# Both state products of the second scan on GpSimd, six state buffers, sums three states behind

## The chip, the cores and the metric

The kernel runs on one core of one Trainium2 chip. The metric is the device time of one execution in microseconds (us). Before the change three runs took 2472.06, 2475.49 and 2479.26 us; their median is 2475.49 us.

In the text PE is TensorE (the matmul engine; PEld its weight loads), DVE is VectorE, ACT is ScalarE, POOL is GpSimd and SP is the engine whose queue issues the DMAs.

## The reference, cut to what matters

A decoder of four layers works on x of shape (4, 256, 256). Each layer has an attention, a cross-attention and a feed-forward part, each added to x and normalised. The first two layers' cross-attentions are selective scans over a context; only the second (layer 1) is meant by "the second attention's loop" here, because its scan runs beside that layer's self-attention:

```python
# layer 1, "xattn": b = 4 batches, l = 256 steps, e = 256 channels, n = 16 states per channel
u     = silu(conv(in_proj(ctx)))                  # (b, e, l)
Bm,Cm = x_proj(u)                                 # (b, 16, l) each
delta = softplus(dt_proj(...) + dt_proj_b)        # (b, e, l)
A     = -exp(A_log)                               # (e, 16)
state_n[t] = state_n[t-1] * exp(delta[t] * A[:, n]) + (delta * u)[t] * Bm[n, t]
y[t]  = sum over n of state_n[t] * Cm[n, t]
out   = (y + D * u) * silu(x_normed)
```

So there are 4 x 16 = 64 scans of 256 channels by 256 steps. Each needs a product with B before it (call it product 1), and a product with C after it (product 2); sixteen results are summed per batch.

## The kernel before

Channels lie on the 128 partitions; a state tile `s` holds 2 x 256 = 512 numbers per partition (two halves of the channels). `Scans._steps` is a generator that the other parts advance: each `next` emits one state. For state (b, n) it emits, in this order:

- L511-512, `add`: the sum of an older state. `late` holds states whose sum has not been emitted; when more than one waits, the oldest is added by a matmul with the identity into a PSUM bank (`ssmps`; two instructions on PE, L500). So sums run two states behind. After n = 15 the bank is folded into `u` (L504).
- L514: a DMA from the SP queue brings row n of B and of C, broadcast to 128 partitions, into `bc` (256 KB; four buffers).
- L518: ACT makes exp(delta A) in one of three `dA` tiles, in two instructions.
- L520: product 1, `s = du * B`, on DVE (helper `tt`, L111), or on POOL (helper `ptt`, L123) when `self.apart` is set.
- L521: the scan on DVE, in place in `s`.
- L529: product 2, `s = s * C`, on DVE (L111).

The tile `s` has four buffers (`wk` has bufs=4); `xd` in the prologue shares its tag. A buffer is free again when PE has summed its state. The `bc` buffer is free again after product 2.

The first scan (layer 0) runs beside the first attention, `run_mqa`, two states per step of its loop, with both products on DVE. The second scan begins in the tail of that; 24 of its states are emitted in layer 0's feed-forward part (L749), 8 in the prologue of the second attention (`run_gqa`, L1031). Then L1035 sets `apart`, and the loop `SmallHeads.run` (L960-972) emits the last 32 states, one per step, with product 1 on POOL.

A step of that loop: PE computes one group of score matmuls for row maxima (`sc`, four instructions; 32 groups in all, 11 of them ahead of the loop) interleaved with one group of transposed scores (`sT`); ACT takes exp of `sT` (`e`); DVE takes two maxima from `sc` (`qn`, L129); then the state of the scan is emitted; then, every second step, PE multiplies `e` with ones and with the values (`o`), and every fourth step DVE takes a reciprocal of 128x256 and a product (`rec`, `oT`, L916). Three PSUM buffers hold `sc`, so PE's next group needs DVE's maxima. For each batch the output projection is added to `x` and normalised (`settle`), and some steps later `gate_pair` (L535) multiplies the scan's `y` by silu(x), transposes the product on PE (L545), adds it to `x` and normalises again. A normalisation asks POOL for the root (`rstd`: L169 and a two-column power through L123), and DVE then scales x (L117). `gate_pair`'s product (L541) is on POOL too. So POOL's queue holds product 1 of the states, the roots and the gate products.

Each engine runs its queue in order. The order in a queue is made when the program is built, by a scheduler that goes by the order of the program, by free buffers and by its own estimates of durations; it may put a later state's work ahead of something that is not ready by its estimate.

Of the kernel before, what the change touches and what calls it, by code (L numbers as in the profile page):

```python
# [19 lines left out]
F32 = mybir.dt.float32  # L20
# [9 lines left out]
ADD, SUB, MUL, MAX, MIN = ALU.add, ALU.subtract, ALU.mult, ALU.max, ALU.min  # L30

P = 128
B, L, D = 4, 256, 256
NT = B * L // P
DC = D // P
# [170 lines left out]
def again(ap, n):  # L206

    return ap.unsqueeze(1).to_broadcast([ap.shape[0], n, ap.shape[1]])
# [189 lines left out]
class Scans:  # L398
# [44 lines left out]
    def _steps(self, pre):  # L443
        K, nc, w, wk = self.K, self.K.nc, self.w[pre], self.wk
        cols = w["cols"]
        N = B * L
        u = self.one.tile([P, DC, N], F32, name="u", bufs=2)
        delta = self.one.tile([P, DC, N], F32, name="delta")
        du = self.one.tile([P, DC, N], F32, name="du")


        taps = []
        for j in range(4):
            t = wk.tile([P, D], F32, name="tap", tag="bc", padded_shape=[P, 2 * L])
            nc.sync.dma_start(out=t, in_=K.A[f"{pre}_cw"][:, j * D : (j + 1) * D].to_broadcast([P, D]))
            K.ptt(t, t, w["in"], MUL)
            taps.append(t)
        for h in range(2):
            for c in range(DC):
                ps = self.bank()  # L460
                for j in range(4):
                    K.mm(ps, taps[j][:, c * P : (c + 1) * P], K.ctxp[:, 2 * h : 2 * h + 2, j : j + L], j == 0, j == 3)
                K.act(u[:, c, 512 * h : 512 * h + 512], ps, AF.Identity, bias=cols[:, c, 0:1])
        K.act(u, u, AF.Silu)
        negA = self.one.tile([P, DC, 16], F32, name="negA")
        K.act(negA, cols[:, :, 2:18], AF.Exp)
        K.ts(negA, negA, -1.0, None, MUL)
        bc = self.dram.tile([2, 16, N], F32, name="bcd")
        for h in range(2):
            s = slice(512 * h, 512 * h + 512)  # L470
            xd = wk.tile([P, 512], F32, name="xd", tag="s")
            ps = self.bank()
            for c in range(DC):
                K.mm(ps[0:40, :], w["xp"][:, c, :], u[:, c, s], c == 0, c == DC - 1)
            nc.scalar.copy(xd[0:40, :], ps[0:40, :])
            for k in range(2):
                nc.sync.dma_start(out=bc[k, :, s], in_=xd[8 + 16 * k : 24 + 16 * k, :])
            for c in range(DC):
                ps = self.bank()
                K.mm(ps, w["dt"][:, c * P : (c + 1) * P], xd[0:8, :])  # L480

                K.ts(delta[:, c, s], ps, cols[:, c, 1:2], None, ADD)
                K.act(du[:, c, s], ps, AF.Abs, bias=cols[:, c, 1:2])
        K.act(du, du, AF.Exp, scale=-1.0)
        K.act(du, du, AF.Ln, bias=K.eps[1.0])
        for c in range(DC):
            K.stt(delta[:, c, :], delta[:, c, :], 0.0, du[:, c, :], MAX, ADD)
            K.ptt(du[:, c, :], delta[:, c, :], u[:, c, :], MUL)

        turn = 0  # L490
        self.y = u

        late = []
        bank = {}

        def add(b, n, s):
            if n == 0:
                bank[b] = self.bank()
            y = bank[b]
            K.mm(y, K.ident, s.rearrange("p c l -> p (c l)"), n == 0, n == 15)  # L500
            if n == 15:
                for c in range(DC):
                    v = u[:, c, b * L : (b + 1) * L]
                    K.stt(v, v, cols[:, c, 18:19], y[:, c * L : (c + 1) * L], MUL, ADD)  # L504
                self.done += 1

        for b in range(B):
            lo = b * L
            for n in range(16):
                yield  # L510
                if len(late) > 1:  # L511
                    add(*late.pop(0))
                t = wk.tile([P, 2, L], F32, name="bc", tag="bc")
                nc.sync.dma_start(out=t, in_=bc[:, n, lo : lo + L].unsqueeze(0).to_broadcast([P, 2, L]))  # L514
                dA = self.dA[turn % 3]
                turn += 1
                for c in range(DC):
                    K.act(dA[:, c, 1:L], delta[:, c, lo + 1 : lo + L], AF.Exp, scale=negA[:, c, n : n + 1])  # L518
                s = wk.tile([P, DC, L], F32, name="s")
                (K.ptt if self.apart else K.tt)(s, du[:, :, lo : lo + L], again(t[:, 0, :], DC), MUL)  # L520
                nc.vector.tensor_tensor_scan(  # L521
                    out=s.rearrange("p c l -> p (c l)"),
                    data0=dA.rearrange("p c l -> p (c l)"),
                    data1=s.rearrange("p c l -> p (c l)"),
                    initial=0.0,
                    op0=MUL,
                    op1=ADD,
                )
                K.tt(s, s, again(t[:, 1, :], DC), MUL)  # L529
                late.append((b, n, s))  # L530
        for t in late:
            add(*t)
# [1907 lines left out]
```

## Time and profile before

| | |
|---|---|
| median of three runs | 2475.49 us (2472.06 to 2479.26) |
| the profiled execution | 2469.83 us |
| its span | 2468.1 us |
| mean granted TensorE clock | 0.948 |
| PE busy over the span | 2265.7 us (92%) |
| DVE busy | 1457.9 us (59%) |
| ACT busy | 801.0 us (32%) |
| POOL busy | 383.2 us (16%) |
| the 32 products 1 on POOL | first at 576.9 us, last at 734.4 us |
| the 128 scans (both layers) | first at 86.5 us, last at 735.7 us |

The span is the time between the first and last instruction of the profiled execution; 1.7 us of its time lie outside. "Busy" of PE is the union of its matmuls, whose ends are modelled. The granted clock is what the throttle let TensorE have; 1.00 is full speed.

### The profile page before, as it was taken

Reading aid. Unit: us, or ns where it says so; the run is one execution under the profiler, and the core shown is the slowest. Engines: PE = TensorE matmul, PEld = TensorE weight load, DVE = VectorE, ACT = ScalarE, POOL = GpSimd, SP = SyncE. Lnnn points to the kernel's source line nnn. Section 1 sums busy time; section 2 is a strip of 40 time slices with the busy share of each in tenths; the row PEclk is TensorE's granted clock in tenths of the full one; section 3 lists DMA queues with packets and bytes.
Section 4 is the critical chain, followed back from the end, with each engine's and each line's share of the span. In section 5 each row is a group of like instructions: output and inputs, shape, how many; then the busy total and the mean of one; then the engine's idle time right before and its main releaser. Section 6 shows DMA issues by size and latency. Waiting matters only on the chain. (4 is left out here: it accounts for less than half of the span.)

```text
span 2468.1 us, 28762 instructions
## 1 busy us (share of the span) xinstructions
PE 2265.7 (92%) x10624; PEld 1521.6 (62%) x10624; DVE 1457.9 (59%) x2920; ACT 801.0 (32%) x1781; POOL 383.2 (16%) x521
## 2 busy tenths in 40 slices
PE   8889998659986999899999999999999988899997
PEld 4466664325434655536888888888776543476774
DVE  3799983788875211280455444444556677774566
ACT  4567663523441111162211111111122243343434
POOL 2221214132330322200011000100210002100001
PEclk9999997778887999999999999999988899999999
DMA  6222221322213544220222112110100002100000
GB/s 201 60 60 59 53 52 35 70 48 50 52 39 101 164 131 127 78 77 9 73 82 87 45 46 73 45 63 31 46 22 1 20 18 71 41 1 1 1 1 18
DMA packets 132836, 138.99 MB, mean 56 GB/s; under 512 B 13876, under 2 KB 120726, under 8 KB 130904
## 3 DMA queue, kind: packets, MB, share of 16 engines
q1 hardware_dynamic: 132696, 137.16, 19.1%
q8 instruction: 84, 1.38, 0.2%
q14 instruction: 56, 0.46, 0.1%
HBM read 134.27 MB, written 2.85 MB: 56 GB/s over the span
## 5 line engine op out<-in xcount | busy, mean ns | idle before, releaser
L132 PE MATMUL ps<-xw,xcT 128*128 128x256 f32 (+1 forms) x2304 | 518.9, 382 | 0.3 <-ACT YT L126 0.3
L132 PEld LDWEIGHTS ps<-xw,xcT 128*128 128x128 f32 x2304 | 430.8, 190 | 64.0 <-issue 1.9
L132 PE MATMUL sc<-kT,qT 32*128 32x256 f32 (+2 forms) x1024 | 239.1, 403 | 11.7 <-DVE qn L129 11.3
L132 PEld LDWEIGHTS sc<-kT,qT 128*128 128x128 f32 (+1 forms) x1024 | 151.7, 200 | 89.7 <-issue 53.5
L111 DVE TENSOR_TENSOR xp<-ps,xb 128x256 f32<-128x256 f32 x96 | 40.4, 421 | 229.7 <-PE ps L132 229.6
L521 DVE TENSOR_TENSOR_SCAN s<-dA,s 128x512 f32<-128x512 f32 x128 | 160.2, 1266 | 15.4 <-POOL s L123 15.3
L132 PE MATMUL ssmps<-s,idz 128*128 128x512 f32 x256 | 142.8, 664 | 24.9 <-DVE s L111 24.0
L126 ACT ACTIVATE dA<-delta,negA 128x255 f32<-128x255 f32 x256 | 116.6, 501 | 133.7 <-DVE s L521 133.6
L126 ACT ACTIVATE p<-sc,nm 128x256 f32<-128x256 f32 (+1 forms) x256 | 111.8, 444 | 101.5 <-DVE nm L129 96.3
L111 DVE TENSOR_TENSOR hT<-u,a 128x512 f32<-128x512 f32 x48 | 33.2, 691 | 186.1 <-PE u L132 186.1
L132 PE MATMUL o<-pT,vt 128*128 128x256 f32 (+1 forms) x352 | 115.0, 449 | 15.5 <-ACT pT L332 15.1
L126 ACT ACTIVATE sq<-xp 128x1024 f32<-128x1024 f32 x24 | 25.4, 1057 | 314.3 <-DVE xp L111 314.3
L129 DVE TENSOR_REDUCE qn<-sc 128x2 f32<-128x480 f32 (+1 forms) x192 | 87.1, 506 | 40.1 <-PE sc L132 38.4
L123 POOL TENSOR_TENSOR xp<-xp,rn 128x128 f32<-128x128 f32 x96 | 35.2, 403 | 476.9 <-DVE rn L1408 476.9
L126 ACT ACTIVATE e<-sT 128x512 f32<-128x512 f32 x128 | 70.2, 590 | 107.7 <-PE sT L132 106.5
L129 DVE TENSOR_REDUCE nm<-sc 128x2 f32<-128x512 f32 (+1 forms) x128 | 76.7, 612 | 45.8 <-PE sc L132 45.5
L1476 DVE TENSOR_TENSOR_SCAN dec<-xT,idz 128x256 f32<-128x256 f32 (+1 forms) x192 | 89.8, 536 | 22.1 <-DMA xT<-ad 22.1
L132 PE MATMUL sT<-q,kT 32*128 32x256 f32 (+1 forms) x384 | 98.7, 501 | 1.7 <-ACT e L126 1.5
L169 POOL TENSOR_SCALAR rstd<-mv 128x2 f32<-128x2 f32 x48 | 11.7, 245 | 555.1 <-DVE mv L161 545.2
L126 ACT ACTIVATE a<-g 128x512 f32<-128x512 f32 x48 | 28.7, 597 | 206.9 <-PE g L132 206.8
L132 PE MATMUL g<-xT,wj 128*128 128x512 f32 x192 | 92.1, 603 | 0.7 <-ACT rows L100 0.7
L123 POOL TENSOR_TENSOR hT<-hT,sel 128x512 f32<-128x512 f32 x48 | 60.7, 1267 | 202.1 <-DVE hT L111 101.1
(504 smaller groups left out, 4133.2 us busy)
## 6 DMA issues: line engine op xcount, KB each, us to landing
bc<-bcd SPq DMA_DIRECT2D x128, 256.0 KB, 4.6
xw<-in_l2a_xw_dram SPq DMA_DIRECT2D x24, 768.0 KB, 4.9
xT<-ad SPq DMA_DIRECT2D x12, 1024.0 KB, 4.6
wj<-in_l1f_gate_dram SPq DMA_DIRECT2D x48, 128.0 KB, 2.5
wj<-in_l1f_up_dram SPq DMA_DIRECT2D x48, 128.0 KB, 2.8
wj<-in_l1f_down_dram SPq DMA_DIRECT2D x48, 128.0 KB, 2.9
sel<-cwd SPq DMA_DIRECT2D x32, 192.0 KB, 3.1
sel<-cwd SPq DMA_DIRECT2D x32, 128.0 KB, 3.2
```

Of the source, the lines that this page charges most:

```text
L111: self.nc.vector.tensor_tensor(out=out, in0=a, in1=b, op=op)
L123: self.nc.gpsimd.tensor_tensor(out=out, in0=a, in1=b, op=op)
L126: self.nc.scalar.activation(out, in_, func, **kw)
L129: self.nc.vector.tensor_reduce(out=out, in_=in_, axis=AX.X, op=op, **kw)
L132: self.nc.tensor.matmul(out, lhsT=lhsT, rhs=rhs, start=start, stop=stop)
L169: self.nc.gpsimd.tensor_scalar(out=out, in0=in_, scalar1=add, scalar2=None, op0=ADD)
L521: nc.vector.tensor_tensor_scan(out=s.rearrange("p c l -> p (c l)"), data0=dA.rearrange("p c l -> p (c l)"), data1=s.rearrange("p c l -> p ...
L1476: nc.vector.tensor_tensor_scan(out=dec[:, k, h, :], data0=ap[:, h, at(bb, k, j) : at(bb, k, 2)], data1=K.idz[:, 0 : (2 - j) * P], initial=0.0,
```

## The change

Inside the second attention's loop (where `apart` is set) product 2 goes to POOL as product 1 does, and a state's sum is emitted three states later, not two. The tile `s` has six buffers, not four; since the buffers are the pool's, this holds for both scans, from the first attention on. `xd` shares the tag and gets the same number. Elsewhere both products stay on DVE and sums stay two states behind.

```diff
@@ Scans._steps
-            xd = wk.tile([P, 512], F32, name="xd", tag="s")
+            xd = wk.tile([P, 512], F32, name="xd", tag="s", bufs=6)
...
-                if len(late) > 1:
+                if len(late) > (2 if self.apart else 1):
                     add(*late.pop(0))
...
-                s = wk.tile([P, DC, L], F32, name="s")
-                (K.ptt if self.apart else K.tt)(s, du[:, :, lo : lo + L], again(t[:, 0, :], DC), MUL)
+                s = wk.tile([P, DC, L], F32, name="s", bufs=6)
+                product = K.ptt if self.apart else K.tt
+                product(s, du[:, :, lo : lo + L], again(t[:, 0, :], DC), MUL)
                 nc.vector.tensor_tensor_scan(
...
-                K.tt(s, s, again(t[:, 1, :], DC), MUL)
+                product(s, s, again(t[:, 1, :], DC), MUL)
                 late.append((b, n, s))
```

## The prediction

> **What bounds the kernel now.** I read the page first: PE is busy 92% of the span, and all 32 states that the change moves lie between 576.9 and 735.7 us. Then the windows view, cut at the stages:
>
> ```profile
> core 0: us, PE busy (x) PEld busy (x) DVE busy (x) ACT busy (x) POOL busy (x), PEclk, DMA share, GB/s
> 86.00:330.00 244.00, 216.86 (x926) 149.12 (x925) 238.34 (x353) 159.80 (x454) 48.50 (x37) 0.99 0.24 59
> ...
> 577.00:690.00 113.00, 108.72 (x689) 54.42 (x688) 94.36 (x137) 48.29 (x96) 33.08 (x30) 0.88 0.24 55
> 690.00:747.00 57.00, 49.01 (x292) 19.37 (x288) 39.37 (x57) 24.55 (x44) 19.02 (x18) 0.88 0.13 32
> ```
>
> In the first attention (86 to 330 us) DVE is full, 238.34 of 244 us. In the second (577 to 747 us) PE is: 157.7 of 170 us, against 133.7 for DVE and 52.1 for POOL. So at most 12.3 us, PE's idle time, can be had there, unless the clock changes: it was granted at 0.88, and halved stretches moving about are worth some us either way. Next the waits between 575 and 740 us (us in total, times, longest):
>
> ```profile
> POOL s L123 <- PE ssmps L132: 89.5, 25, 15.9
> ...
> DVE s L521 <- POOL s L123: 15.3, 14, 2.3
> ...
> DVE x L117 <- POOL rstd L123: 5.1, 5, 1.1
> ...
> PE sc L132 <- DVE qn L129: 4.2, 6, 1.2
> ...
> PE ps L545 <- POOL gate L123: 3.3, 1, 3.3
> ```
>
> POOL's long wait is for a free buffer: product 1 starts when PE has summed the state four before it. DVE's scan waits for that product; the maxima queued behind the scan make PE wait, but for 4.2 us only. The timeline, engine by engine, shows one turn:
>
> ```profile
> 604.16 1.12 PE L132 MATMUL ssmps<-s,idz 128*128 128x512 f32 x2
> 604.26 1.29 DVE L129 TENSOR_REDUCE qn<-sc 128x2 f32<-128x512 f32 x2 [0.33 <-PE sc L132]
> ...
> 605.37 1.26 POOL L123 TENSOR_TENSOR s<-du,bc 128x512 f32<-128x512 f32 x1 [3.42 <-PE ssmps L132]
> ...
> 606.66 1.22 DVE L521 TENSOR_TENSOR_SCAN s<-dA,s 128x512 f32<-128x512 f32 x1 [1.11 <-POOL s L123]
> ...
> 607.92 0.69 DVE L111 TENSOR_TENSOR s<-s,bc 128x512 f32<-128x512 f32 x1
> ```
>
> Sum ends (605.28), product 1 to 606.63, scan to 607.88, product 2 to 608.61, and only then the next maxima (608.53). PE's groups abut all the while: a pair of steps takes from 602.24 to 610.06, 7.8 us or 3.9 us a step at full clock, without a gap.
>
> **The change part by part.** *Product 2 leaves DVE*: 32 x 0.69 = 22 us off DVE. This is not on PE's path except where maxima are late. *It goes to POOL*: no row has it there; product 1 has the same shape and kind, two SBUF inputs of 128x512, 1.27 us (1.26 to 1.68 in all rows). From below, DVE's 0.69; from above, 1.68. I take 1.27: POOL gets 32 x 1.27 = 41 us, 93 of 170.
>
> *A collision*, from the timeline near 645 us:
>
> ```profile
> 645.54 1.27 POOL L123 TENSOR_TENSOR s<-du,bc 128x512 f32<-128x512 f32 x1
> 645.61 1.68 DVE L117 TENSOR_SCALAR x<-x,mv,rstd 128x256 f32<-128x256 f32 x2 [1.14 <-POOL rstd L123]
> ...
> 648.02 1.26 POOL L123 TENSOR_TENSOR gate<-gate,u 128x512 f32<-128x512 f32 x1 [1.21 <-ACT gate L126]
> ...
> 648.40 1.96 DVE L521 TENSOR_TENSOR_SCAN s<-dA,s 128x512 f32<-128x512 f32 x1
> ```
>
> A scan beside a POOL product took 1.96 us against its usual 1.22, losing 0.74 of the 0.88 us that they shared; the two scalings of x took 1.68, and 0.73 at 740.12 with POOL idle. The maxima, read from PSUM, took 1.28 for two beside a product at 613.79, no more than alone. So I count two products and a scan of a state one after the other: 2 x 1.27 + 1.22 = 3.76 us. PE's step is 3.9: it fits, by 0.14. The Trainium skill, "SBUF — State Buffer", section "SBUF: two separate sides", goes further: VectorE operations with two SBUF inputs, or in a two-port mode, and GpSimd share an exclusive port pair, and the loser waits for the whole instruction. By the rule a state takes the full 3.76 us whatever the order; by the row 0.14 of each 0.88 us shared is kept, some 3.6 us, so the fit in PE's step would be 0.14 by the one and 0.3 by the other. It speaks against the change: products on POOL do not run free beside DVE's scans.
>
> *One turn again.* With six buffers and sums three behind, product 1 may again start when the sum of that step ends, now one state further ahead; the same lock-step. Counted from 604.26 (0): product 1 1.1 to 2.4, scan to 3.6, product 2 on POOL to 4.9, the next product 1 (free at 4.1 by PE) to 6.2, its scan to 7.4. Before, DVE came free of that second turn at 7.5 (611.06 + 0.69). So POOL's second turn comes 0.8 us later and gives back the 0.69 that DVE saves: zero, from -0.7 if the scheduler puts the next product 1 first, to +0.7 if it slips another half product. PE hides both signs unless a step is short of slack.
>
> *Reciprocal steps.* Pairs with `rec` and `oT` (2.17 us on DVE) took 9.3 us (610.06 to 619.37) for 7.8 plus 0.4 of transposes: PE loses 1.1 us, five times up to 700 us. `o` ends at 610.16, before the new scan can start: the reciprocal may now go first, and the maxima come 1.1 us earlier. Gain 0 to 5.5 us; I take 2, since DVE's order decides.
>
> *POOL's other work.* Behind product 2, which waits for a scan, POOL's queue holds the next product 1, six roots (0.22 + 0.71) and three gate products. DVE's x (L117), then ACT's gate, then PE's transposes (L545) wait for those. A root can meet a product just begun: 0 to 1.27 us; a product starting behind it can hold x for 0.95 (1.68 - 0.73), as twice or three times already. Charged to PE where it stalls on the gate, three times: 3 x (0 to 2.2) = 0 to 6.6; I take 3.
>
> *The last steps.* After 690 us no maxima remain. Undisturbed, PE's pair of steps took 7.0 us (722.00 to 728.96, with a projection of 1.0), 3.0 to 3.5 a step, less than POOL's 3.76. Over 11 states that is 11 x 0.3 to 0.7, 3 to 8 us; three states of lead (3 x 3.76 = 11 us) and the stalls at the gate cover it. Charge 0, 8 without cover.
>
> *Sums three behind*: the same 64 matmuls; one more at the tail, 1.1 us, while PE at 747 waits for the last gate anyway: zero, 1.1 uncovered.
>
> *The `bc` load* now waits for POOL: on SP nothing urgent stands behind it before 747 us. The state multiplied at 608.34 freed its tile at 611.75, the fourth after it was multiplied at 625.47: 13.7 us for a load of 4.6. Two us later is hidden; zero.
>
> *Six buffers in the first attention*: DVE idle is 5.7 of 244 us, so reordering gains at most that and can lose as much by an earlier scan before a maximum; I take 0.
>
> Sum: -2 + 3 = +1 us on 2469.83, of a size with nothing. On the median of the runs, 5.7 us above the profiled execution: 2476. A measurement of this kernel can tell about 0.3%, 7.4 us, from no change.
>
> **The rivals.** *Slower:* the queue of POOL paces. It decides if products and scan take more than PE's step, 3.9 us, that is, if each state slips by over 0.14 us; then the scan stands blocked in DVE's queue with the maxima or the reciprocal behind it and PE stops. Price: six roots at 2.2 us = 13, or the uncovered last steps 8 with the gates' 6.6; 8 to 20 us in all, 2484 to 2495. For: 3.76 is close to 3.9, and DVE already waits 1.1 us for POOL in every second step. Against: at half clock PE's steps are twice as long, and three states of lead absorb a slip.
>
> *Faster:* DVE's 22 us do reach PE. Then the reciprocals give 5.5 and the other gaps before `sc` and the gate part of the 12.3 us: -8 to -12, 2463 to 2468. For: DVE had 79% to carry, and its order loosens. Against: PE has only 12.3 us to give, and 6 of them sit in gate chains that POOL lengthens.
>
> *It does not do what it says:* the scheduler keeps the states two ahead, since `dA` has three tiles; then the lead is not there but neither is the collision, within 3 us of now; counted with no change.
>
> **How the numbers follow.** No change 0.50, with its own range 2469 to 2483 (2476 -+ 7); slower 0.29; faster 0.21. The range from 2463 to 2493 leaves out the far end of the slower case and what no row shows.
>
> **What would show it.** Right: after, `s<-s,bc` on POOL 32 times at about 1.27 us; DVE busy between 577 and 747 down some 22 us; PE's busy sum there unchanged near 158 us, the stretch 170 -+ 7; POOL's wait for `ssmps` replaced by waits for scans; DVE's wait for `s` above 15 us. Wrong: PE's waits for `qn` or for the gate growing past 15 us (slower), or gone (faster); a shift of over 5 us before 575 us, which I charge nothing.

## The result and the profile after

The changed kernel takes 2481.86 us in the median of 22 runs (2474.33 to 2499.15); the kernel before takes 2475.28 us beside it (22 runs, 2467.87 to 2483.35). The ratio is 1.0036, with a 95% interval of 1.0020 to 1.0052: some 9 us slower in the mean (6.6 between the medians), a little over what can be told from no change. The profiled execution took 2492.25 us, its span 2490.5, at a granted clock of 0.935; before it was 2469.83 us at 0.948.

So a part of the distance between the two profiles is the clock. Over all timed runs of this study, compared within each kernel, the time rises by 0.32 us for each us of half-speed clock (half-speed time being 2 x (1 - granted clock) x span; correlation 0.95, a scatter of 2.2 us left). Where a difference "at equal clock" is given below, that slope has been taken out of the mean of the timed runs. For the change it is +7.2 +- 0.5 us, so the clock accounts for 1.7 us of the difference in the mean and not for the rest. (The 22 runs of before that were taken beside the change have no clock on record. At equal clock every kernel is compared with the 111 runs of before that were taken with the experiments, in four sets that agree within 0.8 us.)

The windows view of the changed kernel, cut as before (columns: window, its length, busy us and instructions of PE, PEld, DVE, ACT and POOL, granted clock, DMA share, GB/s):

```profile
core 0: us, PE busy (x) PEld busy (x) DVE busy (x) ACT busy (x) POOL busy (x), PEclk, DMA share, GB/s
86.00:330.00 244.00, 219.45 (x918) 151.80 (x919) 237.01 (x352) 158.88 (x450) 48.64 (x37) 0.97 0.25 60
577.00:690.00 113.00, 106.59 (x633) 53.92 (x635) 80.69 (x114) 46.00 (x94) 61.69 (x53) 0.83 0.27 53
690.00:747.00 57.00, 49.54 (x269) 20.06 (x266) 30.41 (x46) 25.21 (x44) 31.16 (x29) 0.84 0.16 34
```

In the second attention DVE fell from 133.7 to 111.1 us and POOL rose from 52.1 to 92.9: the products moved as the sum had it. PE's instructions in the same windows fell, from 689 to 633 and from 292 to 269: it is behind, as its loop began some 4 us later (first `sT` at 587.2 after 583.3 us) and had a lower clock (0.83 after 0.88). The waits between 575 and 740 us (us in total, times, longest):

```profile
POOL s L123 <- DVE s L522: 39.3, 27, 2.9
DVE s L522 <- POOL s L123: 35.0, 21, 4.0
POOL s L123 <- PE ssmps L132: 18.9, 12, 5.2
...
PEld sc L132 <- DVE qn L129: 11.3, 12, 4.6
...
POOL s L123 <- DMA bc<-bcd: 8.3, 1, 8.3
...
DVE x L117 <- POOL rstd L123: 5.3, 4, 1.4
...
PE sc L132 <- DVE qn L129: 4.5, 4, 3.1
```

POOL and DVE now wait for each other, 39.3 and 35.0 us; POOL's wait for a summed buffer fell from 89.5 to 18.9. PE's total wait for maxima is what it was (PE 4.5 after 4.2), but the longest is 3.1 us after 1.2. And there is one wait of 8.3 us that was not there: POOL for a row of B and C. One turn in the timeline, DVE and POOL:

```profile
617.22 1.22 DVE L522 TENSOR_TENSOR_SCAN s<-dA,s 128x512 f32<-128x512 f32 x1 [1.11 <-POOL s L123]
...
618.36 1.26 DVE L129 TENSOR_REDUCE qn<-sc 128x2 f32<-128x512 f32 x2
...
618.52 1.28 POOL L123 TENSOR_TENSOR s<-s,bc 128x512 f32<-128x512 f32 x1 [1.34 <-DVE s L522]
...
619.77 1.27 POOL L123 TENSOR_TENSOR s<-du,bc 128x512 f32<-128x512 f32 x1
...
621.07 1.23 DVE L522 TENSOR_TENSOR_SCAN s<-dA,s 128x512 f32<-128x512 f32 x1 [1.45 <-POOL s L123]
...
622.21 1.73 DVE L917 RECIPROCAL rec<-o 128x256 f32<-128x256 f32 x1
```

Scan, product 2, next product 1, next scan, one behind the other, as counted. DVE stands for 1.45 us before the second scan, with the reciprocal and two maxima behind it. That is about what it saved by giving the two products away (2 x 0.69).

### The profile page after: what moved, and what is told of

It reads as the page before. It is cut to its first block, busy times and chain, and to the rows that moved or that the text cites. A ratio compares the mean times of both kernels' runs of the same rounds, so it can differ in the third digit from the quotient of the medians.

```text
span 2490.5 us, 28723 instructions
## 1 busy us (share of the span) xinstructions
PE 2293.8 (92%) x10624; PEld 1534.3 (62%) x10624; DVE 1431.9 (57%) x2888; ACT 802.2 (32%) x1781; POOL 424.6 (17%) x553
## 5 line engine op out<-in xcount | busy, mean ns | idle before, releaser
L132 PE MATMUL sc<-kT,qT 32*128 32x256 f32 (+2 forms) x1024 | 246.4, 414 | 11.2 <-DVE qn L129 10.5
L132 PEld LDWEIGHTS sc<-kT,qT 128*128 128x128 f32 (+1 forms) x1024 | 157.0, 208 | 89.6 <-issue 52.0
L132 PE MATMUL sT<-q,kT 32*128 32x256 f32 (+1 forms) x384 | 106.5, 526 | 5.1 <-ACT e L126 5.0
```

The lines of the kernel that those rows point to most:

```text
L132: self.nc.tensor.matmul(out, lhsT=lhsT, rhs=rhs, start=start, stop=stop)
```

## The experiments

Theory at the outset: the loop's steady part is unchanged, and the loss lies at its start and in the first attention, where only the number of buffers changed. Rival: POOL's queue paces the whole loop. Later a second question was added: whether it was the right product that went to POOL.

All in one table. "First attention" is from its first score matmul to its last output projection; "four steps" are two stretches in the middle of the loop that ran at full clock in every kernel (from the 17th to the 33rd matmul of `sT`, and on to the 49th); "PE idle" is the idle time of PE from the first `sT` of the loop to the feed-forward part's first matmul (`w_l1f_router`). These three come from one profile for each kernel; the first two columns from the timed runs. Each ratio is to the runs of before taken beside that kernel.

| kernel | ratio to before (95%) | at equal clock, us | first attention | four steps | PE idle |
|---|---|---|---|---|---|
| before | | 0 +- 0.2 | 355.7 | 17.1, 18.8 | 11.0 |
| the change | 1.0036 (1.0020 to 1.0052) | +7.2 +- 0.5 | 358.4 | 17.1, 18.8 | 13.1 |
| e1 | 0.9994 (0.9970 to 1.0017) | +1.4 +- 0.7 | 355.1 | 17.1, 18.8 | 12.2 |
| e2 | 1.0000 (0.9980 to 1.0021) | +4.7 +- 1.0 | 358.3 | 17.1, 18.8 | 11.9 |
| e3 | 0.9940 (0.9915 to 0.9965) | -5.2 +- 0.4 | 355.6 | 16.3, 18.0 | 8.0 |
| e4 | 1.0065 (1.0037 to 1.0093) | +10.1 +- 0.3 | 360.2 | 17.1, 18.8 | 9.1 |
| e5 | 0.9973 (0.9942 to 1.0004) | +0.3 +- 0.7 | 359.8 | 16.1, 17.9 | 9.6 |
| e6 | 0.9986 (0.9964 to 1.0009) | -4.8 +- 0.6 | 355.2 | 16.1, 17.9 | 8.3 |
| e7 | 1.0035 (1.0006 to 1.0063) | +4.2 +- 0.8 | 359.8 | 17.1, 18.8 | 10.3 |
| e9 | 1.0006 (0.9976 to 1.0036) | +4.7 +- 0.7 | 358.6 | 17.1, 18.8 | 11.9 |
| e10 | 1.0037 (1.0007 to 1.0068) | +6.3 +- 0.5 | 359.8 | 17.1, 18.8 | 12.3 |
| e11 | 1.0040 (1.0014 to 1.0066) | +6.8 +- 0.7 | 355.7 | 17.1, 18.8 | 15.2 |
| e12 | 1.0050 (1.0024 to 1.0075) | +1.3 +- 0.4 | 346.0 | 16.1, 17.9 | 7.3 |
| e13 | 0.9953 (0.9930 to 0.9976) | -8.8 +- 0.7 | 349.2 | 16.1, 17.9 | 8.2 |

**e1, product 2 alone** (before, with product 2 on POOL in the loop; four buffers, sums two behind):

```diff
-                K.tt(s, s, again(t[:, 1, :], DC), MUL)
+                (K.ptt if self.apart else K.tt)(s, s, again(t[:, 1, :], DC), MUL)
```

> Only product 2 of the loop goes to GpSimd; four buffers and sums two behind, as before. Theory (PE paces the middle of the loop, and the loss comes from GpSimd's queue at the start of the loop and around the gate): 0 to 12 us over before, maxima late in the start less than in the changed kernel since only three first products can be early. Rival 1 (every state pays for two products and a scan one after the other): at least the changed kernel's +9 us, likely +12 to +25, because there is less lead. Rival 2 (the six buffers reorder the queues and cost it): no change, within 4 us of before.

Measured: 2474.51 us, ratio 0.9994; four steps to a tenth as before. Moving the product is worth nothing by itself, and costs at most some us. Rival 1, which asked for at least +9 us, falls here: from the fourth state of the loop on, POOL's queue has product 1 and product 2 in turn, as with the change, and the steps take no longer.

**e2, buffers and sums alone** (the change, with product 2 left on DVE):

```diff
-                product(s, s, again(t[:, 1, :], DC), MUL)
+                K.tt(s, s, again(t[:, 1, :], DC), MUL)
```

> Six buffers and sums three behind, but product 2 stays on DVE. Theory: within 4 us of before; first products may still run four ahead at the start, but no second product stands behind them on GpSimd. Rival 1: no change or up to 5 us faster. Rival 2: +9 us, all of the changed kernel's loss.

Measured: 2474.85 us, ratio 1.0000, but at equal clock +4.7, and the first attention 358.3 us where every kernel with four buffers and product 2 on DVE there has 355.1 to 355.7. With e1's +1.4 it makes 6.1 of the change's 7.2 us: the larger part of the loss comes with the buffers and the later sums, not with the product that moved. The clock of the stage does not explain the first attention: e1 and e2 were both granted 0.97 there. It comes from two places of one kind. The first, DVE before, then PE before:

```profile
144.48 1.26 DVE L111 TENSOR_TENSOR s<-s,bc 128x512 f32<-128x512 f32 x2
145.66 1.28 DVE L129 TENSOR_REDUCE nm<-sc 128x2 f32<-128x512 f32 x2
```

```profile
146.76 1.89 PE L132 MATMUL acc<-w_l0a_wout,oT 128*128 128x256 f32 x8
148.84 1.12 PE L132 MATMUL o<-pT,vt 128*128 128x512 f32 x2 [0.19 <-ACT pT L332]
```

And the same place in e2, DVE and PE:

```profile
144.36 1.26 DVE L111 TENSOR_TENSOR s<-s,bc 128x512 f32<-128x512 f32 x2
145.55 1.28 DVE L111 TENSOR_TENSOR s<-du,bc 128x512 f32<-128x512 f32 x2
146.75 0.68 DVE L129 TENSOR_REDUCE nm<-sc 128x2 f32<-128x512 f32 x1
147.36 1.21 DVE L522 TENSOR_TENSOR_SCAN s<-dA,s 128x512 f32<-128x512 f32 x1
148.49 0.66 DVE L129 TENSOR_REDUCE nm<-sc 128x2 f32<-128x512 f32 x1
```

```profile
146.64 1.89 PE L132 MATMUL acc<-w_l0a_wout,oT 128*128 128x256 f32 x8
152.34 1.12 PE L132 MATMUL o<-pT,vt 128*128 128x512 f32 x2 [3.81 <-ACT pT L332]
```

With two more tiles free, DVE takes products 1 of two more states ahead of the maxima `nm` and a scan between the two; the exponentials on ACT that need the maxima come later, and PE stands 3.81 us before `o` instead of 0.19. The second place, PE in e2:

```profile
175.51 2.08 PE L132 MATMUL o<-pT,vt 128*128 128x512 f32 x2 [3.75 <-ACT pT L332]
```

Before had gaps of 1.95, 2.35 and 2.21 us near there (159.07, 171.17, 191.85). From 190 us on e2 is 4.4 us behind before, and 1.7 of these come back after 326 us. The changed kernel has the same two gaps (150.77 to 154.57 us, 3.80, and 3.76 before 177.7). In e2 each was followed by a stretch at a lower clock: 0.66 from 153 to 158 us and 0.64 from 175 to 183, where before was granted 1.00 in the same windows.

**e3, no second product** (before, with product 2 of the loop's 32 states left out):

```diff
-                K.tt(s, s, again(t[:, 1, :], DC), MUL)
+                if not self.apart:
+                    K.tt(s, s, again(t[:, 1, :], DC), MUL)
```

> The kernel before, with product 2 of the loop's 32 states left out (the outputs of layer 1's scan are wrong in it): DVE is 22 us lighter and GpSimd has no more to do. This is the most that moving product 2 off DVE can bring. Theory: 2 to 6 us faster, since PE had 12 us of idle time and half of it is in gate chains. Rival 1 says the same or more, up to 12 us faster. If it is not faster at all, DVE's relief was never worth anything.

Measured: 2463.06 us, ratio 0.9940. All that a move of product 2 could bring in the loop, with product 1 left on POOL, is 12 us in the mean, 5 at equal clock, with four steps at 16.3 and 18.0. The gain is there to be had; the change does not get it.

**e4, six row buffers** (the change, with six tiles for the rows of B and C; `tap` in the prologue shares their tag):

```diff
-            t = wk.tile([P, D], F32, name="tap", tag="bc", padded_shape=[P, 2 * L])
+            t = wk.tile([P, D], F32, name="tap", tag="bc", padded_shape=[P, 2 * L], bufs=6)
...
-                t = wk.tile([P, 2, L], F32, name="bc", tag="bc")
+                t = wk.tile([P, 2, L], F32, name="bc", tag="bc", bufs=6)
```

> The changed kernel with six buffers for the rows of B and C (bc) too, so that the early first products need not wait for a load behind a second product. Theory: GpSimd's one wait of 8.3 us for the load goes and 3 to 6 us of the changed kernel's +9 come back. Rival 1: no change against the changed kernel, +9 us over before. Rival 2: no change or worse.

Measured: 2494.31 us, slower than the change. It answers in part only. At the loop's start the wait is gone; POOL after the change, and in e4:

```profile
582.38 1.26 POOL L123 TENSOR_TENSOR s<-du,bc 128x512 f32<-128x512 f32 x1 [0.96 <-PE ps L789]
591.91 1.63 POOL L123 TENSOR_TENSOR s<-du,bc 128x512 f32<-128x512 f32 x1 [8.27 <-DMA bc<-bcd]
593.50 6.77 POOL L123 TENSOR_TENSOR s<-s,bc 128x512 f32<-128x512 f32 x4
```

```profile
585.23 6.31 POOL L123 TENSOR_TENSOR s<-du,bc 128x512 f32<-128x512 f32 x4
592.70 1.63 POOL L123 TENSOR_TENSOR s<-s,bc 128x512 f32<-128x512 f32 x1 [1.16 <-DVE s L522]
```

After the change, POOL holds four products 1 in a row; the fourth waits 8.27 us for its row, and products 2 of states already scanned stand behind it. DVE queues three scans meanwhile, and the maxima behind these:

```profile
591.26 5.50 DVE L522 TENSOR_TENSOR_SCAN s<-dA,s 128x512 f32<-128x512 f32 x3
596.68 1.26 DVE L129 TENSOR_REDUCE qn<-sc 128x2 f32<-128x512 f32 x2
```

```profile
597.40 1.23 PE L132 MATMUL sc<-kT,qT 32*128 32x256 f32 x4 [3.07 <-DVE qn L129]
```

PE stands 3.07 us. In e4 PE has no idle time in the loop's first four steps (3.1 us with the change, 0.5 before). But the two tiles more also changed the order ahead of the loop: from the end of the first attention to the loop PE is idle 68.2 us, 53.0 with the change, and that stretch is 8.8 us longer. The whole time is no measure of the row buffers.

**e5, product 1 back on DVE** (the change, product 1 on DVE throughout, product 2 on POOL in the loop; six buffers, sums three behind):

```diff
-                product(s, du[:, :, lo : lo + L], again(t[:, 0, :], DC), MUL)
+                K.tt(s, du[:, :, lo : lo + L], again(t[:, 0, :], DC), MUL)
```

> The changed kernel with the loop's product 1 back on DVE; product 2 stays on GpSimd, six buffers, sums three behind. DVE and GpSimd carry as much as before the change, but no scan waits for GpSimd. Theory S (the loss sits in the start of the loop, where GpSimd takes four first products, waits 8.3 us for the row load of the fourth and keeps three second products behind it): the burst is gone, so 3 us slower to 8 us faster than before. Rival P (every state is paced by product, scan, product on GpSimd): 5 to 12 us faster than before, since that chain is broken for all 32 states.

Measured: 2468.48 us, ratio 0.9973; at equal clock 6.9 us below the change and level with before (+0.3). Four steps take 16.1 and 17.9 us: 1 us less in each. The time does not choose between S and P: some 5 us below before in the mean reaches into the ranges of both.

**e7, the first four on DVE** (the change, product 2 of the loop's first four states on DVE):

```diff
+        self.second = 0
...
-                product(s, s, again(t[:, 1, :], DC), MUL)
+                self.second = self.second + 1 if self.apart else 0
+                (K.ptt if self.second > 4 else K.tt)(s, s, again(t[:, 1, :], DC), MUL)
```

> The changed kernel, but product 2 of the first four states of the loop stays on DVE; the other 28 go to GpSimd as in the change. S: the +9 us go back to within 4 us of before, and the first four steps of the loop (first sT group to the fifth) take 22 to 25 us as before, not 29. P: still at least +7 us, as 28 of 32 states are as in the change.

Measured: 2484.26 us, ratio 1.0035, no better than the change by its time. At equal clock 3.0 us of the 7.2 are gone, and PE's idle time in the first four steps is 1.5 us instead of 3.1. These steps took 25.3 us (29.1 with the change, 22.4 before), but at three different clocks (0.60, 0.56, 0.70). The start of the loop carries a few us; by the ratio alone that would not be seen.

**e9, sums two behind** (the change, sums as before):

```diff
-                if len(late) > (2 if self.apart else 1):
+                if len(late) > 1:
```

> The changed kernel with sums two states behind: six buffers, both products on GpSimd. S: as the changed kernel, +5 to +10 us, because the four early first products stay; the sums were charged nothing. If the loss came from the later sums, it is back at 0. P: +9 us or more, since PE now also meets sums whose second product is late.

Measured: 2478.48 us, ratio 1.0006, with an interval that takes in both kernels; +4.7 at equal clock. The third state of lead brings no gain. Whether it costs something isn't settled.

**e10, product 2 a state later** (the change, with product 2 of a state issued behind product 1 of the next):

```diff
-                if len(late) > (2 if self.apart else 1):
+                if len(late) > 1:
...
-                product(s, s, again(t[:, 1, :], DC), MUL)
-                late.append((b, n, s))
+                if self.apart:
+                    if held:
+                        hb, hn, hs, ht = held.pop()
+                        K.ptt(hs, hs, again(ht[:, 1, :], DC), MUL)
+                        late.append((hb, hn, hs))
+                    held.append((b, n, s, t))
+                else:
+                    K.tt(s, s, again(t[:, 1, :], DC), MUL)
+                    late.append((b, n, s))
...
```

> The changed kernel with product 2 issued one state later (after product 1 of the next state) and sums two behind from there, so a sum stands three states behind as in the change. GpSimd then need not wait for the scan between its two products. P: 5 to 10 us faster than the changed kernel. S: within 4 us of the changed kernel, as the burst and the load at the start stay.

Measured: 2483.15 us, ratio 1.0037, four steps at 17.1 and 18.8. But the order of the program did not become the order of the queue. In the trace POOL's products stand as with the change: four products 1, four products 2, then one of each in turn, and product 2 still waits for the scan of the product 1 just before it:

```profile
617.45 1.26 POOL L123 TENSOR_TENSOR s<-du,bc 128x512 f32<-128x512 f32 x1 [1.97 <-PE ssmps L132]
620.05 1.29 POOL L123 TENSOR_TENSOR s<-s,bc 128x512 f32<-128x512 f32 x1 [1.34 <-DVE s L523]
621.29 1.29 POOL L123 TENSOR_TENSOR s<-du,bc 128x512 f32<-128x512 f32 x1
623.92 1.27 POOL L123 TENSOR_TENSOR s<-s,bc 128x512 f32<-128x512 f32 x1 [1.34 <-DVE s L523]
```

So e10 is nearly the change over again, in its order and in its time (+6.3 beside +7.2 at equal clock). Whether the order of the two products on POOL matters is not shown by any run.

**e6, one product on each, four buffers** (before, with the two products changing places):

```diff
-                (K.ptt if self.apart else K.tt)(s, du[:, :, lo : lo + L], again(t[:, 0, :], DC), MUL)
+                K.tt(s, du[:, :, lo : lo + L], again(t[:, 0, :], DC), MUL)
...
-                K.tt(s, s, again(t[:, 1, :], DC), MUL)
+                (K.ptt if self.apart else K.tt)(s, s, again(t[:, 1, :], DC), MUL)
```

> Four buffers, sums two behind; in the second attention's loop product 1 is on DVE and product 2 on POOL. Theory (the change loses in two places: the two further buffers cost 3 to 4 us in the first attention, and the burst at the start of the loop some more; in the loop DVE's wait for product 1 costs PE about 1 us in four steps): from the first score matmul of the first attention to its last output projection 355 to 356 us as before (358.35 with the change); four steps in the middle of the loop at full clock 16.1 and 17.9 us as with six buffers and the same division (17.1 and 18.8 before); time 3 to 8 us below before. Rival (it was the two further buffers that let PE go faster in those four steps): 17.1 and 18.8 us as before, time within 3 us of before.

Measured: 2472.52 us, ratio 0.9986; no change by the ratio, -4.8 at equal clock; first attention 355.2, four steps 16.1 and 17.9. The gain in the steps comes from which product is on POOL, not from the buffers. DVE at the reciprocal, the place shown above for the change:

```profile
607.52 0.87 DVE L111 TENSOR_TENSOR s<-du,bc 128x512 f32<-128x512 f32 x1
608.49 1.22 DVE L521 TENSOR_TENSOR_SCAN s<-dA,s 128x512 f32<-128x512 f32 x1
609.63 1.73 DVE L916 RECIPROCAL rec<-o 128x256 f32<-128x256 f32 x1
611.40 0.42 DVE L111 TENSOR_TENSOR oT<-o,rec 128x256 f32<-128x256 f32 x1
611.74 1.28 DVE L129 TENSOR_REDUCE qn<-sc 128x2 f32<-128x512 f32 x2
```

No wait stands in these lines: product 1 feeds DVE's own scan, and product 2 only the sum, which nobody waits for at once. The reciprocal starts 2.0 us after the end of the maxima, 2.6 with the change. (Before it was 1.9 us; there the wait, 1.11 us, stood ahead of the scan before, at 606.66.)

**e11, six buffers in the loop only** (the change; the two further tiles have a tag of their own):

```diff
-            xd = wk.tile([P, 512], F32, name="xd", tag="s", bufs=6)
+            xd = wk.tile([P, 512], F32, name="xd", tag="s")
...
+                third = self.apart and n % 3 == 2
-                s = wk.tile([P, DC, L], F32, name="s", bufs=6)
+                s = wk.tile([P, DC, L], F32, name="s", tag="s2" if third else "s", bufs=2 if third else 4)
```

> The change as it is, but the two further buffers are a tag of their own that only states of the second attention's loop use (every third state); the other states keep four. Same memory, same engines, sums three behind in the loop. Theory (the two further buffers cost the first attention 3 to 4 us by letting DVE run scans ahead of its maxima): the first attention back from 358.35 to 355 to 356 us, and 3 to 4 us of the 7 us that the change loses at equal clock come back; the start of the loop stays as slow as with the change. Rival (the loss in the first attention is of the memory's place, not of the number of buffers): 358 to 360 us there, and the time of the change, 6 to 9 us above before.

Measured: 2484.97 us, ratio 1.0040. One half came as expected: the first attention is back at 355.7 us with as many tiles in all, so the loss there is of the number of buffers. But the time did not follow (+6.8 at equal clock where about 4 was due): PE is idle 15.2 us in the loop, 5.3 of them in the first four steps. Why this way of sharing the tiles costs more there is left open.

**e12, product 2 on POOL for all 128 states** (e6 without its condition):

```diff
-                K.tt(s, s, again(t[:, 1, :], DC), MUL)
+                K.ptt(s, s, again(t[:, 1, :], DC), MUL)
```

> Four buffers, sums two behind; product 1 on DVE and product 2 on POOL for all 128 states, so in the first attention too, where DVE was busy 238.34 of 244 us and POOL 48.5. Theory (what counts is which engine is full in the stage: DVE there, PE in the second attention): 64 products of 0.69 us, 44 us, leave DVE in the first attention; a scan beside a product on POOL loses 0.74 of 0.88 us shared, so that up to 64 x 0.74 = 47 us come back at worst; the first attention takes 325 to 350 us instead of 355.65, and the time falls by 5 to 30 us. Rival (DVE and POOL share so much that a product moved gains nothing where DVE is full): 354 us or more there and a time within 5 us of before, or above.

Measured: 2488.47 us, ratio 1.0050, slower by the time, +1.3 at equal clock; yet the first attention took 346.0 us, 9.7 less. The groups between 86 and 375 us, before and in e12 (busy us, mean ns):

```profile
L111 DVE TENSOR_TENSOR s<-du,bc 128x512 f32<-128x512 f32 x63 | 61.0, 998 | 0.3 <-PE ssmps L132 0.2
...
L111 DVE TENSOR_TENSOR s<-s,bc 128x512 f32<-128x512 f32 x64 | 41.7, 676 | 0.4
```

```profile
L123 POOL TENSOR_TENSOR s<-s,bc 128x512 f32<-128x512 f32 x64 | 105.3, 1662 | 65.3 <-DVE s L521 39.7 <-PE sc L132 13.3 <-PE ps L330 6.1
...
L111 DVE TENSOR_TENSOR s<-du,bc 128x512 f32<-128x512 f32 x62 | 75.5, 1250 | 0.7 <-PE ssmps L132 0.3
```

41.7 us left DVE; products 1 beside POOL's grew by 14.5, a third of it, and POOL's took 1662 ns instead of 1.27 us. What was gained was lost behind it, where 24 states run in the feed-forward part. The waits between 372 and 580 us:

```profile
PEld ssmps L132 <- POOL s L123: 27.3, 13, 3.5
...
PE ssmps L132 <- POOL s L123: 17.0, 12, 3.5
```

PE waits in order for sums whose product 2 comes late from POOL: from the end of the first attention to the loop it takes 232.7 us (211.0 before), 70.7 of them idle (56.8), at a granted clock of 0.75 (0.79). Over the timed runs, too, e12 has 31 +- 6 us more half-speed time than before, so its figure at equal clock leaves out a cost that may be the edit's own.

**e13, product 2 on POOL where it gained** (e12, but on DVE for the states between):

```diff
-                K.ptt(s, s, again(t[:, 1, :], DC), MUL)
+                (K.ptt if self.apart or pre == "l0x" else K.tt)(s, s, again(t[:, 1, :], DC), MUL)
```

> Four buffers, sums two behind, product 1 on DVE for all states; product 2 on POOL in the first attention (all 64 states of the first scan) and in the second attention's loop (32 states), and on DVE for the 32 states between, in the feed-forward part and the prologue. Theory (with product 2 on POOL for all states the first attention gained 9.7 us, and the 32 states between lost it again, as PE waited for sums and rope behind POOL): first attention 346 us, from there to the loop about 210 us as before (232.7 with all on POOL), the loop 155 to 162 us; time 6 to 16 us below before. Rival (what the first attention gains is lost behind it whatever POOL does there, to the clock or to loads): the part between takes 217 us or more and the time is within 5 us of before.

Measured: 2462.81 us (2447.05 to 2478.65), ratio 0.9953 (0.9930 to 0.9976): faster than the kernel before by 11 us in the mean and 8.8 at equal clock, and than the change by more. The part between is back at 213.1 us with 55.8 idle. The first attention took 349.2 in this profile, not 346. The windows view:

```profile
86.00:330.00 244.00, 221.88 (x948) 153.97 (x949) 221.95 (x306) 162.11 (x467) 140.32 (x96) 0.97 0.28 59
```

DVE, which was full there (238.34), has room, and PE does 948 matmuls in the window instead of 926.

## Why the prediction was right, and where not

The forecast of about 2476 us (2463 to 2493) stands 6 us below what was measured; 2481.86 is inside the likeliest case's own range (2469 to 2483), at its upper end, though the ratio's interval starts above no change. The sum of +1 missed +7 at equal clock. That the forecast came so near owes something to luck, as two of its terms were wrong in opposite directions.

*One turn and the steady loop: right.* Priced at zero, measured at zero: 17.1 and 18.8 us, with the mechanism as told, since DVE loses by waiting for POOL (35.0 us, above the 15 foreseen) what it saves. Product 2 on POOL took 1.33 us in the mean, against 1.27 charged.

*Reciprocal steps: not the 2 us charged as a gain.* The loss of about 1 us was read rightly (`o` ended at 610.13, not 610.16, which changes nothing), and e3, e5 and e6 show that it can be had (17.1 to 16.1). The change gets nothing of it, because the scan still stands ahead of the reciprocal and now waits 1.45 us for product 1.

*POOL's other work: not the 3 us charged as a cost.* DVE's `x` waits 5.3 us for the roots (5.1 before); PE's gap before the transposes of the last gate product is 3.46 us (3.34 before), and an earlier one of 3.06, which ended with ACT's `q`, shrank to 0.76. Two terms that were both wrong, this one and the reciprocal's, cancelled but for 1 us.

*Last steps and sums: zero was not contradicted.* The gap at the end stays, as just said; e9 shows no gain of the third state of lead.

*The `bc` load: wrong at one place.* "Two us later is hidden" was worked out from the steady state. At the loop's start the further buffers let POOL take four products 1 at once, ahead of the products 2 that free rows, and it waited 8.27 us. PE's idle time in the first four steps rose from 0.5 to 3.1 us.

*Six buffers in the first attention: the mis-sized term.* The prediction bounded it by 5.7 us either way, named an earlier scan before a maximum as what could cost, and took 0. It costs 2.7 us with the change (358.4 - 355.7), and 2.7 to 4.5 in the seven kernels with six buffers from the start, all of which have the two gaps shown at e2 (3.8 us, and 3.8 to 4.6). On an engine full to 238 of 244 us, work that can start earlier starts in somebody else's place; there was no reason for the middle of the range.

*The slower rival,* POOL's queue pacing the loop, does not hold in the steady part: e1 has the same chain on POOL and stands at +1.4 us, and the eight steps at full clock are as long as before, with as little idle time of PE (0.8 us in both). *The faster rival* does not either: DVE's 22 us did not reach PE. *It does not do what it says* falls too: 32 products 2 ran on POOL.

What stays open: the first attention and the loop's idle time give 2.7 + 2.1 us of the 7.2. In the change's profile the loop also ran at half speed for 56.5 us instead of 41.0, and took 175.6 us instead of 164.7, more than the 7 us that the prediction allowed the stretch. Over the kernels this share moves between 34 and 65 us with one profile each, so whether the edit moves the throttle in the loop or it fell so in that execution can't be said. Over the timed runs the whole kernel's half-speed time is 5 +- 6 us above before, so no shift is shown there.

The Trainium skill, "SBUF — State Buffer", section "SBUF: two separate sides", lets a VectorE operation with two SBUF inputs and GpSimd exclude each other for a whole instruction. In the loop the rule had nothing to decide, since DVE's scans and POOL's products took turns anyway. In the first attention of e12 the rows agree with it within some 0.1 us: a POOL product that began 0.05 us ahead of DVE's took 1.26 us, as alone (at 130.18), and one that began 0.05 us behind took 1.77 (at 139.22), while the pair of DVE products beside them took 2.37 and 2.36 us, against 1.28 in e2 at 145.55. DVE came out ahead all the same: 271.0 us busy fell to 252.9 between 86 and 375 us.

## What to carry to other kernels

Ask not only how much work leaves an engine, but on which side of that engine's own instructions it stood: a product that feeds the engine's next instruction comes back as a wait, one whose result goes to a patient reader can be given away. More buffers are a change of order, on every loop that shares the pool: where an engine was full, they let later work step in front of what somebody waited for. And read in the trace whether an edit to the order of the program reached the queue: in e10 it did not. Give work to the slower engine stage by stage, where the profile shows its old engine full and nobody waiting for the new one.

## What the runs showed of the hardware

The time of one and the same kernel follows the granted clock closely, 0.32 us for each us at half speed: the changed kernel's own 22 runs spread over 25 us, more than three times the effect looked for. Comparing means at equal clock made differences of 3 us readable that the ratios alone left unclear. But half-speed time differs between kernels too (31 us more in e12, 21 less in e3, each +- 6 to 7), and what an edit does to the clock is then taken out with the rest.

PE's busy time hides waits. In four steps e6 gains 1.0 us, but only 0.4 us of idle time was to be seen there before; the other 0.6 us is busy time, though the durations of the matmuls add up to the same within 0.1 us (52.95 and 52.84). Matmuls that start late overlap the modelled ends of those before them, so groups that abut are no proof of an engine without slack.
